# A Householder step with fewer matmuls, GpSimd rows and a planner that weighs layouts, in a four-layer graph network

## The chip, the cores and the metric

The kernel runs on one core of one Trainium2 chip. The metric is the device time of one execution in microseconds (us); three runs of the kernel before took 2328.39, 2328.72 and 2331.53 us. All data are float32. Of the engines, PE multiplies matrices (a matmul first loads one operand into the array as weights, then streams the other through it), DVE does vector arithmetic, ACT does functions and scaled copies, POOL (GpSimd) is a third vector engine, and SP issues DMAs.

## The reference, cut to what matters

Four layers run one after the other on x (128 batches x 64 nodes x 256 features) with one 64x64 graph matrix `adj`. The change touches the work that is done during layer 0.

```python
# layer 0: graph convolution, two products, two batch norms over all 8192 rows
h = relu(layernorm(x))
agg = einsum('nm,bmd->bnd', A_hat, h)                 # A_hat: adj + I, scaled
h = relu(batchnorm(agg @ W1.T + b1))                  # 256 -> 512
x = x + batchnorm(h @ W2.T + b2)                      # 512 -> 256
# layer 1: the eigenvectors of a 64x64 Laplacian of adj
L_norm = d_inv_sqrt[:, None] * (diag(deg) - A) * d_inv_sqrt[None, :]
_, U = eigh(L_norm)
h = relu(layernorm(x))
out = relu(einsum('mn,bnd->bmd', U.T, h) @ W1 + b1) @ W2 + b2
x = x + einsum('nm,bmd->bnd', U, out)
# layer 2: two graph products and four LSTMs; layer 3: attention over 512 edges
```

Layer 1 cannot start before the 64x64 eigenvectors U are known. They depend on `adj` alone, so they can be computed beside layer 0.

## The kernel before

**Two jobs at once.** `eigenvectors` runs layer 0 and the eigenproblem together. Layer 0 works on 16 blocks of 512 rows. In the hidden phase (`hidden_block`) a block is normalized by ACT, mixed with the graph by PE (`mix`, sixteen 128-wide matmul passes with the matrix `BDH`), multiplied by W1 (`product`, eight calls of 512 columns), and each result is copied out by ACT and given to DVE for batch statistics. After all 16 blocks the first batch norm's factors are known. Then the features phase (`features0`) goes over the 16 blocks again: ACT scales them, PE multiplies by W2 (eight calls of 512 columns a block), ACT copies out and squares. A float32 call of `matmul` appears in the trace as two MATMUL records, one for each of two passes.

**The eigenproblem.** `tridiagonal` reduces the 64x64 matrix A by 62 Householder steps (`householder`, c from 63 down to 2). After that `vectors` scales the result (`scale`), multiplies the reflectors together (`reflectors`), finds the eigenvalues by two rounds of a 32-step recurrence on DVE (`poly`, `values`), the vectors of the tridiagonal matrix (`twisted`), U itself, and a verdict (`verdict`) on which a branch is taken: where the verdict is bad, a slow solver runs in its place.

**One Householder step.** Each row is kept on all 64 partitions at once. `zy` makes two products with A: row c-1 of A (`z`) and A times column c (`y`), each a call with 64 weight columns. DVE and ACT form the reflection from the row x: norm by `square`, root `s0`, reciprocal `r`, `tt`, `nb`, then the corrected entries of x and the factor `KAP`. ACT makes `uk = KAP * x`; DVE makes `uA = z * nb + y`, the scalar `c2` (a sum over `uA * uk`), and `v = x * c2 - uA`. `outer` adds uk v' + v uk' in PSUM by two calls with one-row operands, and DVE adds it to A. The next row is made in two DVE operations from `uk`, `v` and `z`, without waiting for PE. A DMA on SP's queue stores each x row in `V`; x has a ring of 8 buffers.

**The planner.** `Plan` decides the order of the three engines' instructions when the program is built. `chain` places a step of the eigenproblem at once, at the time when its inputs are ready by the `busy` and `ready` numbers written beside it; before that, `fill` places waiting pieces of layer 0 (`beside`) on the same engine if they end no later than the slack of that engine after that time (`slack`: 0.6 us on PE, T; 0.3 on ACT, S; 0.3 on DVE, V). `emit` then issues everything in that order, and `Ordered` (line 799) ties each instruction of an engine behind the one before. So each engine runs its list strictly in order, and a late input holds up all that is behind it. Pieces of layer 0 that are left over when the 62 steps are placed (`rest`) are emitted after `vectors` and fill its gaps. The five PSUM banks of layer 0 are part of the plan.

All instructions that pass through `Ordered` carry line 799 in the profile, so they are told apart by their tiles: `ps` is layer 0's PSUM, `fps` and `fvps` that of the eigenproblem, and names that begin with `f_` are the eigenproblem's tiles.

Of the kernel before, what the change touches and what calls it, by code (L numbers as in the profile page):

```python
# [8 lines left out]
F32 = mybir.dt.float32  # L9
I32 = mybir.dt.int32  # L10
AF = mybir.ActivationFunctionType
ALU = mybir.AluOpType
# [772 lines left out]
GRID = 64  # L785

# [56 lines left out]
class Plan:  # L843
# [55 lines left out]

    def rest(self):  # L900

        while any(self.queue.values()):
            for e in self.queue:
                self.fill(e, 1e9)
# [8 lines left out]
class Fast:  # L913
# [31 lines left out]
    def sum(self, out, a, s, b, op0, op1=ALU.mult, name="junk"):  # L945

        w = a.shape[-1]
        j = self.t(f"{name}{a.shape[0]}", a.shape[0], 64)
        self.o.stt(j[:, 0:w], a, s, b, op0, op1, acc=out)
# [3 lines left out]
    def constants(self):  # L953
# [6 lines left out]
        self.P = t("P", 64, 1)  # L960
        iota(self.P[:], [[0, 1]], 0, 1)
# [21 lines left out]
        o.ts(self.low[:], self.J[:64, :], self.P[:], ALU.is_lt)  # L983
# [3 lines left out]
        o.copy(pi[:], self.P[:])  # L987
# [15 lines left out]
    def tridiagonal(self, S, made, plan):  # L1003
# [3 lines left out]
        A = self.A = t("A", 64, 64)  # L1007
# [3 lines left out]
        for x in (KAP, NB, V):  # L1011
            nc.vector.memset(x[:], 0.0)
        s0, r, tt, q, c2 = (t("h_" + x, 64, 1) for x in "s0 r t q c2".split())
        ja = t("ja", 64, 64)
        bc = lambda c, n=64: c.to_broadcast([n, 64])
        now = {}
        go = plan.chain

        def keep(name, a, b):
            now[name] = self.mm((a, b))  # L1020

        d = go("T", lambda: keep("p", S, self.JR[:]), [made], 0.3, 0.5)
        d = go("V", lambda: o.copy(m[:], now["p"][:]), [d], 0.15, 0.28)
        d = go("T", lambda: keep("p", self.JR[:], m[:]), [d], 0.3, 0.5)
        rest = go("V", lambda: o.copy(A[:], now["p"][:]), [d], 0.15, 0.28)
        d = go("T", lambda: keep("p", bc(ident[:64, 63:64]), A[:]), [rest], 0.3, 0.5)

        def first():
            x = now["x"] = self.rows.tile([64, 65], F32, name="f_x", bufs=8)
            o.copy(x[:, 0:63], now["p"][:, 0:63])  # L1030

        def square(w):
            x = now["x"]
            self.act(ja[:, 0:w], x[:, 0:w], AF.Square, accum_out=x[:, w:w + 1])

        row = go("V", first, [d], 0.15, 0.28)
        h = go("S", lambda: square(63), [row], 0.34, 0.42)
        for c in range(63, 1, -1):
            row, h, rest = self.householder(c, now, go, row, h, rest, (s0, r, tt, q, c2), square)

    def householder(self, c, now, go, row, h, rest, scalars, square):

        o, nc, t = self.o, self.nc, self.t
        ident = self.k.ident
        A, NB, OA, KAP, V = self.A, t("NB", 64, 64), t("OA", 64, 64, 2), t("KAP", 64, 64), t("V", 64, 64)
        s0, r, tt, q, c2 = scalars
        bc = lambda a, n=64: a.to_broadcast([n, 64])
        x = lambda a, b: now["x"][:, a:b]
        nb = NB[:, c - 1:c]
        e, w = 0.001 * c, c - 1  # L1050

        def zy():
            now["zp"] = self.ps.tile([64, 64], F32, name="fps")
            nc.tensor.matmul(now["zp"][:, 0:c], bc(ident[0:c, c - 1:c], c), A[0:c, 0:c], start=True, stop=True)
            now["yp"] = self.ps.tile([64, 64], F32, name="fps")
            nc.tensor.matmul(now["yp"][:, 0:c], bc(A[0:c, c:c + 1], c), A[0:c, 0:c], start=True, stop=True)

        def row_z():
            now["z"] = self.rows.tile([64, 64], F32, name="f_z")
            self.act(now["z"][:, 0:c], now["zp"][:, 0:c], AF.Copy)  # L1060

        def row_uk():

            nc.sync.dma_start(V[c:c + 1, 0:c], now["x"][0:1, 0:c])
            now["uk"] = self.rows.tile([64, 64], F32, name="f_uk")
            self.act(now["uk"][:, 0:c], x(0, c), AF.Copy, scale=KAP[:, c:c + 1])

        def row_uA():
            now["uA"] = self.rows.tile([64, 64], F32, name="f_uA")
            o.stt(now["uA"][:, 0:c], now["z"][:, 0:c], nb, now["yp"][:, 0:c], ALU.mult, ALU.add)  # L1070

        def row_v():
            now["v"] = self.rows.tile([64, 64], F32, name="f_v")
            o.stt(now["v"][:, 0:c], x(0, c), c2[:], now["uA"][:, 0:c], ALU.mult, ALU.subtract)

        def outer():
            uk, v = now["uk"], now["v"]
            p = now["p"] = self.ps.tile([64, 64], F32, name="fps")
            nc.tensor.matmul(p[0:c, 0:c], uk[0:1, 0:c], v[0:1, 0:c], start=True, stop=False)
            nc.tensor.matmul(p[0:c, 0:c], v[0:1, 0:c], uk[0:1, 0:c], start=False, stop=True)  # L1080

        def row_x():
            now["x"] = self.rows.tile([64, 65], F32, name="f_x", bufs=8)
            o.stt(x(0, w), now["uk"][:, 0:w], now["v"][:, w:c], now["z"][:, 0:w], ALU.mult, ALU.add)


        z = go("T", zy, [rest], 0.34, 0.42)
        sq = go("S", lambda: self.act(s0[:], x(c, c + 1), AF.Sqrt), [h], 0.13, 0.23)
        oa = go("S", lambda: self.act(OA[:, c, 1:2], x(c - 1, c), AF.Copy), [row], 0.12, 0.22)
        zs = go("S", row_z, [z], 0.15, 0.26 + e)  # L1090
        sg = go("V", lambda: o.ts(q[:], x(c - 1, c), **halve(0)), [row])
        d = go("V", lambda: o.recip(r[:], s0[:]), [sq])
        d = go("V", lambda: o.stt(tt[:], r[:], x(c, c + 1), s0[:], ALU.mult, ALU.add), [d, h])
        b = go("V", lambda: o.mul(nb, q[:], tt[:]), [d, sg])
        d = go("V", lambda: o.stt(x(c - 1, c + 1), OA[:, c, :], nb, x(c - 1, c + 1), ALU.mult, ALU.add), [b, oa])
        d = go("V", lambda: o.recip(KAP[:, c:c + 1], x(c, c + 1)), [d])
        uk = go("S", row_uk, [d], 0.16, 0.32 + e)
        d = go("V", row_uA, [zs, b, z], 0.12 + e, 0.25 + e)
        d = go("V", lambda: self.sum(c2[:], now["uA"][:, 0:c], 0.5, now["uk"][:, 0:c], ALU.mult), [uk, d],
               0.2 + e, 0.28 + e)  # L1100
        v = go("V", row_v, [d], 0.15 + e, 0.26 + e)
        p = go("T", outer, [v], 0.25, 0.45)
        if c > 2:
            row = go("V", row_x, [v], 0.15 + e, 0.22 + e)
            row = go("V", lambda: o.stt(x(0, w), now["v"][:, 0:w], now["uk"][:, w:c], x(0, w), ALU.mult, ALU.add),
                     [row], 0.15 + e, 0.25 + e)
            h = go("S", lambda: square(w), [row], 0.28 + e, 0.36 + e)
        rest = go("V", lambda: o.add(A[0:c, 0:c], A[0:c, 0:c], now["p"][0:c, 0:c]), [p], 0.12 + e, 0.22 + e)
        return row, h, rest

    def reflectors(self):
# [8 lines left out]
        self.sum(kc[:], self.KAPs[:], 1.0, ident, ALU.mult)  # L1120
# [22 lines left out]
    def scale(self):  # L1143

        o, nc, t = self.o, self.nc, self.t
        NB, A = t("NB", 64, 64), self.A
        self.KAPs = t("KAP", 64, 64)
        DM, NE = t("DM", 64, 64), t("NE", 64, 64)
        o.mul(DM[:], A[:], self.k.ident[:64, :64])
# [316 lines left out]
class Kernel:  # L1466
# [340 lines left out]
    def hidden_block(self, i, r, m, plan, needs, used):  # L1807
# [9 lines left out]
        def mix(dc):  # L1817
            p = now["m", dc] = psum.tile([P, BT], F32, name="ps")
            for j in range(TPB):
                self.mm(p[:, j * P:(j + 1) * P], now["h"][:, j, dc * P:(dc + 1) * P], self.BDH[:])  # L1820
# [966 lines left out]
```

## Time and profile before

| what | us |
|---|---|
| median of the three runs | 2328.72 |
| span of the profiled execution, first to last instruction | 2325.1 |
| 0 to 17: loads, graph matrix, first Householder step | 17 |
| 17 to 200: hidden phase beside Householder steps | 183 |
| 200 to 217: last hidden results, batch norm factors | 17 |
| 217 to 272: features phase beside the last Householder steps | 55 |
| 272 to 364.4: features phase beside the rest of the eigenproblem | 92.4 |
| 364.4 to 372: verdict's branch, then layers 1 to 3 | 7.6 |
| 372 to the end: layers 1 to 3 | 1953 |

The span ends 3.6 us below the median of the runs; what lies around it is not in the trace. The page's slices, each 58 us long, show how full the engines are; the first six and a half slices are the stage that is changed:

```profile
DVE  8887676888447777666767676559756686766667
ACT  5765865754436654433444444336435544444321
POOL 0000000000000000000000000000000000000000
PEclk9999999999999999999999999999999999999999
```

Each digit is the busy share in tenths. POOL is idle: over the whole span it has 26 instructions, nearly all of them fills and index patterns at the very start. The clock that PE was granted is nearly full everywhere.

One Householder step took between 2.8 and 6.3 us, 4.19 on the mean (from the starts of the operation that writes `f_h_q`, 11.8 for the first and 267.2 for the last: 255.4 us over 61 steps).

### The profile page before, as it was taken

How to read it: one execution, taken by the hardware profiler on the slowest of the kernel's cores; microseconds unless marked ns; L12 is line 12 of the kernel's file. 1: busy time of each engine (PE TensorE's matmuls, PEld its weight loads, DVE VectorE, ACT ScalarE, POOL GpSimd, SP SyncE). 2: the span in 40 equal slices, each digit the busy share in tenths (PEclk: the TensorE clock that was granted, in tenths of full speed). 3: DMA queues.
4: the chain of work that ended last, by engine and by line, in shares of the span. 5: the costliest groups of instructions: out<-in, count | busy, mean ns of one | idle time of the engine just before them, and what ended most of it. 6: DMA issues, size and time to landing. Idle time of an engine off the chain costs nothing.

```text
span 2325.1 us, 32725 instructions
## 1 busy us (share of the span) xinstructions
PE 2283.6 (98%) x12169; PEld 1633.1 (70%) x12169; DVE 1629.3 (70%) x4054; ACT 1139.5 (49%) x2483; POOL 3.0 (0%) x26
## 2 busy tenths in 40 slices
PE   7999998999999999999999999999999999999999
PEld 4554445676777788888999998888885544554544
DVE  8887676888447777666767676559756686766667
ACT  5765865754436654433444444336435544444321
POOL 0000000000000000000000000000000000000000
PEclk9999999999999999999999999999999999999999
DMA  5000211230000000001000002000010000000001
GB/s 171 1 1 26 65 56 30 71 83 19 1 37 0 1 19 1 1 1 37 1 1 1 1 1 73 1 1 17 1 46 28 1 5 15 15 19 14 14 24 46
DMA packets 61065, 54.81 MB, mean 24 GB/s; under 512 B 15203, under 2 KB 58724, under 8 KB 60900
## 3 DMA queue, kind: packets, MB, share of 16 engines
q1 hardware_dynamic: 60900, 52.66, 7.4%
q8 instruction: 97, 1.59, 0.3%
q14 instruction: 68, 0.56, 0.1%
HBM read 35.86 MB, written 16.78 MB: 23 GB/s over the span
## 4 chain that ended last, share of the span: by engine, by line
PE 79%; DVE 3%; issue 1%; ACT 1%; DMA 0%; SPq 0%; ACTq 0%; DVEq 0%
PE ps L799 69%; PE acc L799 5%; PE pt L799 4%; PE pe L799 1%; PE y L799 1%; DVE aw L799 1%; DVE X L799 1%; DVE sm_m L799 0%; DVE XV L799 0%; ACT ls_g L799 0%; ACT h L799 0%; DVE ls_g L799 0%; ACT big L799 0%; DVE ls_t L799 0%; DVE sm_e L799 0%
## 5 line engine op out<-in xcount | busy, mean ns | idle before, releaser
L799 ACT ACTIVATE ls_g<-ls_g,ls_b 128x512 f32<-128x512 f32 (+4 forms) x472 | 243.1, 565 | 151.4 <-DVE ls_g L799 149.6
L799 ACT ACTIVATE ls_g<-ps,ls_b 128x256 f32<-128x256 f32 (+3 forms) x268 | 115.5, 470 | 330.9 <-PE ps L799 327.7
L799 PE MATMUL ps<-z,w 128*128 128x512 f32 x512 | 254.9, 621 | 0.9 <-ACT z L799 0.9
L799 PE MATMUL ps<-big,X 128*128 128x176 f32 (+3 forms) x848 | 212.7, 366 | 0.1
L799 DVE TENSOR_TENSOR ls_g<-ls_z,ps 128x512 f32<-128x512 f32 (+5 forms) x256 | 146.8, 579 | 91.9 <-PE ps L799 90.4
L799 DVE TENSOR_TENSOR aw<-at,ed_OST 128x1024 f32<-128x1024 f32 x128 | 149.9, 1219 | 83.0 <-PE ps L799 82.8
L799 PE MATMUL ps<-ls_tx,X 128*128 128x160 f32 (+2 forms) x960 | 206.8, 326 | 0.6 <-ACT ls_g L799 0.6
L799 PE MATMUL ps<-X,X 128*128 128x160 f32 (+1 forms) x896 | 199.1, 306 | 0.0
L799 PE MATMUL ps<-X,ls_w 128*128 128x256 f32 x640 | 190.5, 379 | 0.0
L799 PEld LDWEIGHTS ps<-ls_tx,X 128*128 128x128 f32 x960 | 161.8, 190 | 15.1 <-DVE X L799 4.8
L799 PEld LDWEIGHTS ps<-big,X 128*128 128x128 f32 x848 | 145.9, 190 | 29.7 <-issue 19.4
L799 DVE TENSOR_TENSOR X<-ls_g 128x1024 f32<-128x1024 f32 (+2 forms) x108 | 117.4, 1087 | 49.9 <-ACT ls_g L799 49.8
L799 ACT ACTIVATE r<-ps 128x512 f32<-128x512 f32 x256 | 131.6, 614 | 41.5 <-PE ps L799 41.4
L799 PEld LDWEIGHTS ps<-X,X 128*128 128x128 f32 x896 | 148.4, 190 | 0.0
L799 PE MATMUL ps<-X,ls_s 128*128 128x256 f32 x480 | 142.3, 379 | 0.0
L799 PEld LDWEIGHTS ps<-z,w 128*128 128x128 f32 x512 | 87.2, 190 | 69.0 <-issue 60.2
L799 PE MATMUL ps<-ls_tx,ls_s 128*128 128x256 f32 x464 | 134.8, 379 | 0.0
L799 PE MATMUL ps<-ed_S,Q 64*128 64x512 f32 x512 | 132.9, 618 | 1.4 <-DVE hT L799 0.7
L799 PE MATMUL ps<-ls_tx,ls_w 128*128 128x256 f32 x464 | 133.2, 380 | 0.0
L799 PEld LDWEIGHTS ps<-X,ls_w 128*128 128x128 f32 x640 | 121.4, 190 | 16.8 <-DVE X L799 0.3
L799 PE MATMUL ps<-big,ls_w 128*128 128x256 f32 x464 | 131.9, 379 | 0.7 <-ACT ls_z L799 0.7
L799 PE MATMUL ps<-aw,ed_ODT 128*64 128x512 f32 x512 | 117.3, 595 | 0.1
(545 smaller groups left out, 4019.0 us busy)
## 6 DMA issues: line engine op xcount, KB each, us to landing
X<-in_x_dram SPq DMA_DIRECT2D x32, 512.0 KB
xs<-X SPq DMA_DIRECT2D x16, 512.0 KB
X<-xs SPq DMA_DIRECT2D x16, 512.0 KB
out_dram<-X SPq DMA_DIRECT2D x31, 256.0 KB
X<-in_L_gnn_Wih_t_dram SPq DMA_DIRECT2D x4, 512.0 KB
ls_w<-in_L_gnn_Wih_t_dram SPq DMA_DIRECT2D x4, 512.0 KB
ls_w<-in_L_gnn_Whh_t_dram SPq DMA_DIRECT2D x4, 512.0 KB
w<-in_L_gnn_W_t_dram SPq DMA_DIRECT2D x2, 512.0 KB
```

The source lines that it names most:

```text
L799: i = method(*a, **kw)
```

## The change

The planner gets a method `weigh`. It builds the plan of one Householder step with each of 27 sets of slacks (0.2, 0.45, 0.8 on PE; 0.1, 0.3, 0.6 on ACT; 0.1, 0.35, 0.65 on DVE), rates each by the busy time that it placed (weight 1 on PE, 0.5 on ACT, 2 on DVE) less 2.7 times the time at which the step's results are ready, takes the state back, and plans the step once more with the best set. All of this happens while the program is built.

The step's arithmetic is laid out anew. z and y come from one matmul call whose weights `ex` hold two blocks of 64 columns: a column of the identity, written by GpSimd, and the masked column of the new A, written by DVE straight from PSUM (`m`). The rank-two update is one call with 65-row operands: row 0 of `left` holds uk and row 64 of `right` holds uk, both written by GpSimd; row 64 of `left` holds -uA, also by GpSimd; rows 0 to 63 of `right` hold v, written by DVE. It is uneven because v now carries the whole scalar `dd`, and the other side carries uA alone. `tt` goes; `qh` (DVE) and `qs` (ACT) come. `uk` is no longer an input of the sum. The ring of x has 6 buffers in place of 8, and z, uk and uA one each in place of two.

In layer 0 the calls of W1 and W2 are cut into halves of 256 columns and the mix into two pieces of two tiles, with the planner's times to match.

```diff
+R = 65
...
+    def weigh(self, make, slacks, worth, cost):
+        free, queue = dict(self.free), {e: list(v) for e, v in self.queue.items()}
+        n, k = len(self.steps), len(self.opened)
+        best = None
+        for slack in [*slacks, None]:
+            self.slack = slack or best[1]
+            made = make()
+            if slack is None:
+                return made
+            gain = sum(x.busy * worth.get(x.engine, 0.0) for x in self.steps[n:])
+            gain -= cost * max(x.at + x.ready for x in made)
+            if best is None or gain > best[0]:
+                best = gain, slack
...
+        self.MK = t("MK", 64, 64)
+        o.ts(self.MK[:], self.J[:64, :], self.P, ALU.is_gt)
...
+        self.left, self.right = ([t(f"{n}{i}", R, 66) for i in range(2)] for n in ("L", "R"))
+        self.ex = [t(f"EX{i}", R, 2, 64) for i in range(2)]
+        for x in (*self.left, *self.right, *self.ex):
+            nc.gpsimd.memset(x[:], 0.0)
...
+            row, h, rest = plan.weigh(lambda: self.householder(c, now, go, row, h, rest),
+                                      self.slacks, dict(T=1.0, S=0.5, V=2.0), 2.7)
...
+    def unit(self, c):
+        self.nc.gpsimd.tensor_copy(self.ex[c % 2][0:64, 0, :], self.k.ident[0:64, c - 1:c].to_broadcast([64, 64]))
...
-        def zy():
-            now["zp"] = self.ps.tile([64, 64], F32, name="fps")
-            nc.tensor.matmul(now["zp"][:, 0:c], bc(ident[0:c, c - 1:c], c), A[0:c, 0:c], start=True, stop=True)
-            now["yp"] = self.ps.tile([64, 64], F32, name="fps")
-            nc.tensor.matmul(now["yp"][:, 0:c], bc(A[0:c, c:c + 1], c), A[0:c, 0:c], start=True, stop=True)
+        def products():
+            zy = now["zy"] = self.ps.tile([P, 64], F32, name="fps")
+            nc.tensor.matmul(zy[:, 0:c], ex[c % 2][:].rearrange("p a b -> p (a b)"), A[:, 0:c], start=True, stop=True)
...
+        def side(out, a, scale):
+            nc.gpsimd.tensor_scalar(out, a[0:1, 0:c], scale, None, op0=ALU.mult)
...
         def outer():
-            nc.tensor.matmul(p[0:c, 0:c], uk[0:1, 0:c], v[0:1, 0:c], start=True, stop=False)
-            nc.tensor.matmul(p[0:c, 0:c], v[0:1, 0:c], uk[0:1, 0:c], start=False, stop=True)
+            p = now["p"] = self.ps.tile([P, 64], F32, name="fps")[:R]
+            nc.tensor.matmul(p[:, 0:c], left[:, 0:R], right[:, 0:c], start=True, stop=True)
...
-        d = go("V", lambda: o.stt(tt[:], r[:], x(c, c + 1), s0[:], ALU.mult, ALU.add), [d, h])
-        b = go("V", lambda: o.mul(nb, q[:], tt[:]), [d, sg])
+        g = go("V", lambda: o.mul(qh[:], q[:], x(c, c + 1)), [sg, h], 0.09, 0.25)
+        d = go("V", lambda: o.recip(r[:], s0[:]), [sq], 0.09, 0.25)
+        qr = go("S", lambda: self.act(qs[:], s0[:], AF.Copy, scale=q[:]), [sq, sg], 0.13, 0.25)
+        b = go("V", lambda: o.stt(nb, r[:], qh[:], qs[:], ALU.mult, ALU.add), [d, g, qr], 0.09, 0.25)
...
+        uA = go("V", row_uA, [b, zy, zs], 0.12 + e, 0.25 + e)
+        k = go("V", lambda: o.recip(kap, x(c, c + 1)), [d], 0.09, 0.25)
+        uk = go("S", row_uk, [k], 0.16, 0.32 + e)
+        sides = [go("P", lambda: side(left[64:65, 0:c], now["uA"], -1.0), [uA], 0.15, 0.4)]
+        sides += [go("P", lambda out=out: side(out, now["x", c], KAP[0:1, c:c + 1]), [k], 0.15, 0.4)
+                  for out in (left[0:1, 0:c], right[64:65, 0:c])]
+        d = go("V", lambda: self.sum(dd[:], now["uA"][:, 0:c], kap, x(0, c), ALU.mult), [uA, k], 0.2 + e, 0.28 + e)
+        v = go("V", lambda: o.stt(right[0:64, 0:c], x(0, c), dd[:], now["uA"][:, 0:c], ALU.mult, ALU.subtract),
+               [d], 0.12 + e, 0.26 + e)
...
+            row = go("V", row_x1, [uk], 0.12 + e, 0.26 + e)
...
+        p = go("T", outer, [v] + sides, 0.25, 0.45)
...
+            m = go("V", lambda: o.stt(ex[w % 2][0:64, 1, :], now["p"][0:64, w:c].to_broadcast([64, 64]), A[0:64, w:c],
+                                         self.MK[:, w:c].to_broadcast([64, 64]), ALU.add, ALU.mult), [p], 0.12, 0.25)
         rest = go("V", lambda: o.add(A[0:c, 0:c], A[0:c, 0:c], now["p"][0:c, 0:c]), [p], 0.12 + e, 0.22 + e)
+        if c > 3:
+            go("P", lambda: self.unit(c - 2), [zy], 0.15, 0.4)
...
-            plan = Plan(dict(T=0.6, S=0.3, V=0.3), 5)
+            plan = Plan(dict(T=0.6, S=0.3, V=0.3, P=0.0), 5)
...
-            x = beside("T", lambda dc=dc: mix(dc), h, 0.98, 1.1, bank)
+            x = beside("T", lambda dc=dc: mix(dc, 0), h, 0.5, 0.6, bank)
+            x = beside("T", lambda dc=dc: mix(dc, 1), [x], 0.5, 0.66)
...
-            x = beside("T", lambda hc=hc: product(hc, 0), mixed, 0.86, 0.9, bank)
-            x = beside("T", lambda hc=hc: product(hc, 1), [x], 0.86, 1.0)
+            x = beside("T", lambda hc=hc: product(hc, 0, 0), mixed, 0.43, 0.43, bank)
+            for k, kc in ((0, 1), (1, 0), (1, 1)):
+                x = beside("T", lambda hc=hc, k=k, kc=kc: product(hc, k, kc), [x], 0.43, 0.6 if k and kc else 0.43)
...
-                for kc in range(4):
-                    x = beside("T", lambda oc=oc, kc=kc, f=product: f(oc, kc), [z[kc]] + ([x] if x else []), 0.86, 1.0,
-                               None if kc or x else bank)
+                for k in range(2):
+                    for kc in range(4):
+                        x = beside("T", lambda oc=oc, k=k, kc=kc, f=product: f(oc, k, kc), [z[kc]] + ([x] if x else []),
+                                   0.43, 0.6, None if kc or x else bank)
```

## The prediction, made before the changed kernel was run

> **What bounds the kernel now.** I began with the page's slices, which say that PE is nearly always busy, and went on to the windows of layer 0's own matmuls (tile `ps`) by stage, since a busy PE only says that records lie close together. The changed code runs in the first 364 us; everything later takes U and x and is the same in both kernels. This view has, for each stretch, its length and then busy time and number of instructions by engine:
>
> ```profile
> 17.00:200.00 183.00, 156.72 (x500) 73.42 (x501) 41.03 (x60) 53.63 (x92) 1.00 0.10 30
> 200.00:217.00 17.00, 14.78 (x70) 8.67 (x68) 2.79 (x4) 2.39 (x4) 0.92 0.00 0
> 217.00:272.00 55.00, 48.05 (x94) 15.46 (x94) 1.40 (x2) 14.31 (x40) 1.00 0.26 76
> 272.00:364.40 92.40, 76.76 (x163) 28.54 (x162) 0.00 (x0) 28.09 (x80) 1.00 0.16 47
> ```
>
> The first bracket counts PE's records: layer 0 still had 163 of them to do when the last Householder step ended near 272. Then I read one step in the order of PE's time (start, duration, engine):
>
> ```profile
> 102.60 1.45 PE L799 MATMUL ps<-z,w 128*128 128x512 f32 x3
> 103.98 0.27 PE L799 MATMUL fps<-f_v,f_uk 1*44 1x44 f32 x2
> 104.09 0.25 PE L799 MATMUL fps<-f_uk,f_v 1*44 1x44 f32 x2
> 104.26 1.13 PE L799 MATMUL ps<-z,w 128*128 128x512 f32 x2
> 105.32 0.31 PE L799 MATMUL fps<-f_A,ident 43*64 43x43 f32 x2
> 105.46 0.29 PE L799 MATMUL fps<-f_A 43*64 43x43 f32 x2
> 105.67 1.55 PE L799 MATMUL ps<-z,w 128*128 128x512 f32 x3
> ```
>
> Durations overlap, so I use start to start. A 512-wide pass takes 0.429 us (eight from 100.35 need 3.63 up to 103.98, less 0.20 for the change). `outer` holds PE 0.28 us (103.98 to 104.26), `zy` 0.35 (105.32 to 105.67). The two passes between them need 0.86 but 1.06 goes by: each change from layer 0 to the eigenproblem and back loses 0.20. A step costs PE about 0.28 + 0.35 + 2 x 0.20 = 1.03 at this c, 0.98 on the mean of all.
>
> The sum from layer 0's first pass (17.3) to the verdict's matmul (364.3) is 347 us:
> - layer 0: 512 passes of 0.429, 256 + 56 narrow ones (mix, and the fills of the batch norm's gap) of 0.109: 253.
> - 62 steps of 0.98: 61.
> - the rest of the eigenproblem after 272, read in the same way: 26.
> - the remainder, 7, is PE standing; listing the holes gives about 12, 9 of them before 272 (1.5 before 197.4, 1.3 at 200 under a lower clock, 3 in the steps at 93.7, 114.3 and 215.9, in which no layer 0 work lay between the two visits) and 3 at 334 and 348; the steps without layer 0 work saved some changes in return.
>
> So **PE is the bound of this stage**, not the length of the Householder chain. Both end together, but only because the planner stretches a step: the chain by its own hops (start to start where nothing stood between: square 0.35, root 0.23, `r` 0.20, `tt` 0.24, `nb` 0.26, x 0.24, KAP 0.24, `uk` 0.36, sum 0.24, v 0.29, two row operations 0.58) needs 3.2 us, and a step takes 4.19. PE waits for nothing in between.
>
> **The change part by part.**
>
> *One call in place of two for z and y.* The saving seems obvious: half the calls. But the one call has 128 weight columns where two had 64 each. The trace has such shapes elsewhere:
>
> ```profile
> 358.94 0.43 PE L799 MATMUL fvps<-U,I 64*128 64x64 f32 x2
> 359.30 0.70 PE L799 MATMUL ps<-z,w 128*128 128x512 f32 x1
> ...
> 313.15 0.38 PE L799 MATMUL fps<-f_v_L,f_I 64*128 64x1 f32 x2
> 313.46 1.13 PE L799 MATMUL ps<-z,w 128*128 128x512 f32 x2
> ...
> 279.74 0.32 PE L799 MATMUL fps<-f_VT 64*64 64x64 f32 x2
> 279.99 1.12 PE L799 MATMUL ps<-z,w 128*128 128x512 f32 x2
> ```
>
> With 128 weight columns a call holds PE 0.36 us at 64 streamed columns and 0.31 at one; `zy` took 0.37 at c = 60 and 0.32 at c = 2. **PE gains nothing**: 62 x 0.01, under 1 us.
>
> *One call for the update.* 65 weight columns and 65 rows are nearest to the third pair: 0.25 at 64 columns, less 0.05 for short ones as above. Before, `outer` took from 0.36 (c = 61) to 0.17 (c = 2). Mean 0.23 against 0.24: again under 1 us. Together -1.
>
> *The chain.* `tt` and `uk` leave the path from row to row: 0.24 + 0.36, and one of the two row operations (`row_x1`) no longer waits for v: 0.29. So 3.2 becomes 2.3. The other loop (update, `m`, add to A, `products`, `zs`, `uA`, sum, v) adds to about 2.1 to 2.6 by the same hops, as `m` comes in front of the add. I expect steps of 2.8 to 3.6 us and an end of the 62 steps near 200 to 235 instead of 272. It buys little: the passes of layer 0 that no longer fit between the steps run after them. The gain would be the whole 37 to 70 us only if PE had nothing left to do.
>
> *More work on DVE and ACT.* Per step one DVE operation more (`m`, some 0.27, near `uA`'s 0.25; `qh` replaces `tt`), one more on ACT (`qs`, near OA's 0.19). Hidden under PE's time: DVE is 80% busy in the hidden phase and ACT 67%. Without cover it is 0.27 + 0.1 a step on the chain, which still leaves it under 3 us.
>
> *GpSimd rows.* Three one-row operations a step, two needed with v by `outer`, and `unit` beside. No POOL operation of this kind is in the trace. Nearest: the affine select that reads and writes 128 elements, 0.30 us; a fill of 1 to 4 elements 0.09; below. A row has 32 elements on the mean, so I take 0.2, with 0.09 and 0.56 (an index pattern of 512) as ends. They follow each other on POOL: three need 0.6, and a hand-over as between DVE and ACT (0.23) gives 0.85 after uA; sum and v need 0.55. The planner counts 0.7.
>
> ```profile
> 1.11 0.30 POOL masks.py:199 TENSOR_SCALAR_AFFINE_SELECT ident<-ident 128x128 f32<-128x128 f32 x1
> ```
>
> Here a rule speaks against the change. The Trainium skill, "SBUF — State Buffer", section "Who interferes with whom", says that a DVE instruction with two SBUF inputs and a GpSimd instruction that reads SBUF exclude each other: the later one waits for the whole of the other. The sum and v are such instructions and run just when the rows are copied. By the row alone the rows cost the chain 0.15 beyond the plan; by the rule DVE also waits about 2 x 0.2, 0.55 in all, 34 us over 62 steps if it lay open. No overlap of the two engines is in this trace. What covers it: the planner books 0.25 + 0.25 of PE for a step, and the trace shows 0.97, so PE will run 0.47 us a step later than planned, and a chain that is up to that much late makes no hole. I take 0 to 5 us, and 1 for the sum.
>
> *A ring of six.* The ring of x shrinks to 6, and the SP queue frees it: the first row's DMA into V stands behind the loads and starts at 34.88. The seventh row reuses its slot. Six steps of about 4 us from 11.5 (these first ones carry statistics on DVE) come to 35: a wait of 0 to 3, I take 1. Single buffers for z, uk and uA are read out within a step: 0. The fills of the new tiles run before the graph matrix is ready (8.66): 0.
>
> *Finer pieces.* 512 passes become 1024 of 256 columns. These run at 0.215 in layer 2 (twelve in 2.75 us with the last one's tail): 512 x (2 x 0.215 - 0.429) = +1. In return a visit of the eigenproblem waits behind a piece of 0.43 in place of 0.86. The 27 layouts cost nothing on the chip.
>
> *Holes.* With a shorter chain the visits' inputs come earlier, and I take it that 6 of the 9 us of holes up to 272 close (an estimate: two thirds); those of 334 and 348 belong to later code.
>
> **Sum:** calls -1, GpSimd rows +1, ring +1, pieces +1, holes -6: -4 us. On the execution profiled 2325.1 becomes 2321; with the 3.6 us around it, **2324.5** against the median 2328.7.
>
> **Rivals.**
> - *Slower: the GpSimd rows set the step.* Place: `outer`, first in PE's queue with all of layer 0 behind it. If a row takes d, it is ready 3d + 0.25 after uA, 0.7 is planned and 0.47 absorbed: the point is d = 0.31 us. At 0.4 PE stands 0.28 a step, 17 us, so 2342; at 0.56 far more, +47. For it: the lock, and the weights, which reward short steps and so plan no reserve. Against: the 0.30 row moved four times as much.
> - *More: PE's holes all close.* All 12 us instead of 6, -10 us in all: 2318.6; the 2 us of costs gone as well: 2316. For it: the list of holes; against: two lie behind matmuls of the unchanged part. PE cannot give more.
> - *The gap between the phases loses its cover.* Now 202 to 217 holds four steps. If steps are 3 us, 62 of them are over before the hidden phase, and the gap falls among `poly`'s operations on DVE. Then 5 to 10 us of PE are empty: 2335.
> - *It does not do what it says*: the uneven update upsets the verdict and the slow solver runs. Nothing in the trace tells; the time would be beyond any range here.
>
> **How the numbers follow.** PE's sum 0.50 (own range 2317 to 2333), GpSimd rows 0.27, all holes 0.11, uncovered gap 0.10, slow solver 0.02. The range that keeps 8 in 10: 2313 to 2350. I call 0.2% (4.7 us) the least difference that can be told. PE's sum gives 0.25 faster, 0.21 same, 0.04 slower; the holes add 0.11 faster; the gap 0.02 same, 0.08 slower; the rows 0.01 same, the rest slower. Rounded: faster 0.36, same 0.24, slower 0.40.
>
> **What would show it.** Right: the last `f_h_q` well before 267, `products` holding PE 0.31 to 0.36 and `outer` 0.20 to 0.25, layer 0's last pass still near 360. Wrong: PE waiting for POOL or DVE before `outer`, steps over 3.8 us, or the verdict's branch starting well before 355, which would mean that PE was never the bound.

## The result and the profile after

| | median, us | range |
|---|---|---|
| before | 2328.66 | 2328.39 to 2331.53 |
| changed | 5582.39 | 5580.53 to 5584.05 |

The ratio is 2.3971 (95% interval 2.3937 to 2.4004). From the page of the kernel before, the busy time by engine:

```profile
PE 2283.6 (98%) x12169; PEld 1633.1 (70%) x12169; DVE 1629.3 (70%) x4054; ACT 1139.5 (49%) x2483; POOL 3.0 (0%) x26
```

And from the page of the changed kernel the span, the same row, two rows of slices and the costliest group:

```profile
span 5580.8 us, 57110 instructions
...
PE 2359.0 (42%) x12738; PEld 1775.8 (32%) x12738; DVE 4338.0 (78%) x23282; ACT 1317.7 (24%) x3353; POOL 85.8 (2%) x282
...
PE   8871100000000000000000000099999999999999
...
PEclk9985555555555555555555555599999999999999
...
L122 PE MATMUL eps<-e_left,e_ones 64*64 64x1 f32 x2 | 0.4, 252 | 2179.3 <-DVE e_left L45 2179.3
```

DVE has 23282 instructions where it had 4054, and the tiles `e_...` belong to the slow solver: **the verdict came out bad and the branch of the slow solver ran**. The windows of all engines show how long (length, then busy time and instructions of PE, its weight loads, DVE, ACT and POOL, then PE's clock):

```profile
10.00:384.00 374.00, 331.74 (x1733) 266.90 (x1733) 287.61 (x1431) 248.81 (x811) 81.78 (x248) 0.98 0.15 44
384.00:3626.00 3242.00, 83.97 (x321) 46.59 (x321) 2690.32 (x19173) 166.04 (x814) 0.11 (x1) 0.50 0.00 0
3626.00:5580.00 1954.00, 1942.16 (x10682) 1461.60 (x10681) 1353.30 (x2631) 901.41 (x1727) 0.63 (x3) 1.00 0.06 18
```

The middle row is 3242 of the 3254 us. It has 19173 DVE instructions, and PE is busy for 84 us of it. The rows of layer 0's matmuls (tile `ps`), in the stretches that the prediction used, say that the first stage did not get shorter either:

```profile
17.00:200.00 183.00, 149.72 (x708) 118.94 (x709) 39.72 (x58) 50.86 (x88) 0.97 0.11 30
200.00:217.00 17.00, 12.79 (x49) 9.15 (x48) 2.65 (x4) 3.42 (x6) 0.80 0.01 1
217.00:272.00 55.00, 43.24 (x193) 30.20 (x192) 3.50 (x5) 8.31 (x23) 1.00 0.14 39
272.00:364.40 92.40, 78.01 (x324) 58.46 (x323) 0.00 (x0) 28.12 (x84) 1.00 0.22 63
```

PE's time with layer 0 between 17 and 272 us fell from 219.6 to 205.8 us (sums of the first three rows), its clock from 0.92 to 0.80 in the second row and from 1.00 to 0.97 in the first. The last Householder step ends near 280 instead of 272, and a step takes 4.38 us instead of 4.19. So there are two questions: why the verdict fell, and what the changed schedule costs without the slow solver.

### The profile page after: what moved, and what is told of

Read it like the earlier page. It is cut to its first block, busy times and chain, and to the rows that moved or that the text cites. A ratio compares the mean times of both kernels' runs of the same rounds, so it can differ in the third digit from the quotient of the medians.

```text
span 5580.8 us, 57110 instructions
## 1 busy us (share of the span) xinstructions
PE 2359.0 (42%) x12738; PEld 1775.8 (32%) x12738; DVE 4338.0 (78%) x23282; ACT 1317.7 (24%) x3353; POOL 85.8 (2%) x282
## 5 line engine op out<-in xcount | busy, mean ns | idle before, releaser
L457 ACT ACTIVATE e_q_r_y<-e_q_r_hh 64x1 f32<-64x1 f32 x540 | 109.6, 203 | 1357.3 <-DVE e_q_r_hh L51 1234.7
L800 PE MATMUL ps<-z,w 128*128 128x256 f32 x1024 | 259.3, 399 | 0.2
L68 DVE RECIPROCAL e_q_r_r<-e_q_r_y 64x1 f32<-64x1 f32 x540 | 83.6, 155 | 153.6 <-ACT e_q_r_y L457 150.9
L800 PEld LDWEIGHTS ps<-z,w 128*128 128x128 f32 x1024 | 189.9, 195 | 25.3 <-ACT z L800 1.4
L800 PEld LDWEIGHTS ps<-big,X 128*128 128x128 f32 x848 | 146.0, 190 | 29.7 <-issue 19.4
```

Source lines behind the costliest of these rows:

```text
L68: self.v.reciprocal(o, a)
L457: nc.scalar.activation(y[:], hh[:], AF.Sqrt)
L800: i = method(*a, **kw)
```

## Why the slow solver ran: ten kernels

Theory L: only the rounding of the tridiagonal matrix changed. In `twisted` each eigenvector is built outward from one row r, the one with the smallest |g|. g is made of ratios of float32 determinants, which for some eigenvalues cancel to exact zeros towards the end of the recurrence; then row 0 can have g = 0 by accident and be chosen although the vector has next to nothing there. Rival D: the uneven update, or a row written by GpSimd, makes the vectors inexact for good.

The first kernel multiplies the verdict by zero (`o.ts(li[:], p[:], 0.0, ALU.mult)` in place of the copy), so that the slow solver never runs.

> The changed kernel with its verdict multiplied by zero, so the vectors of the fast solver are used whatever the tests say (left out: the decision itself; the tests still run). Theory A, the +3254 us are the slow solver and nothing else: the time falls to near the kernel before. The last matmul of the verdict starts at 371.5 us in the profile of the changed kernel and at 364.35 in that of before, and nothing behind it was changed, so 2328.7 + 7.2 = 2336, between 2332 and 2341. Theory B, something outside the slow solver (the layers behind, the clock) pays too: more than 2345. The prediction's own sum, without the slow solver: 2324.5.

Measured: 2344.23 us (2341.18 to 2346.03) against 2326.56, ratio 1.0067 (1.0049 to 1.0084). The 3240 us are the slow solver, as theory A said. The number is 3 us over its interval, since I had read the wrong landmark. The output of this kernel is off by 0.047 (relative error), so the vectors were really bad, and the verdict was not merely too strict. The verdict's matmul moved from 364.35 to 373.66, but layer 0's last pass, which came just before it, now comes after it: 383.7 instead of 363.8. What follows starts at 392.8 instead of 373.5.

The next two leave the verdict in force. One swaps the factors of one sum in one step:

```diff
-self.sum(dd[:], now["uA"][:, 0:c], kap, x(0, c), ALU.mult)
+self.sum(dd[:], x(0, c), kap, now["uA"][:, 0:c], ALU.mult)     # c == 20 alone
```

> The changed kernel with the two factors of one sum swapped in one of the 62 steps (c = 20: x * kap * uA in place of uA * kap * x); same instructions, same order, other rounding in the last bits. Theory L, the verdict falls by a rounding accident in one row of the twisted factorization: another rounding draws another lot, the fast vectors pass, and the time is that of the held verdict, 2332 to 2341. Theory D, the uneven update (asymmetric halves, rows through GpSimd) costs accuracy in a lasting way, or a row is wrong: one swapped product in one step cannot mend it, 5582.

The other keeps row 0 from being chosen:

```diff
         o.mabs(g[:], g[:])
+        nc.vector.memset(g[:, 0:1], 8.0)
         o.red(gm[:], g[:], ALU.min)
```

> The changed kernel with one instruction more: the column 0 of g, the measure by which a vector's twist row is chosen, is set to 8, so that row 0 is never chosen. Theory L says which accident it is: for one eigenvalue the determinants of the reversed sequence have rounded to exact zeros, g of row 0 is an exact 0.0, and row 0 is chosen though this vector has hardly anything there; barred, the verdict passes and the time is that of the held verdict within 0.5 us, 2332 to 2341. Theory D: the vectors are inexact as a whole, the verdict stays bad, 5582.

Measured: 2346.51 us (one run) and 2345.58 us (2344.1 to 2345.9, ratio 1.0075, 1.0059 to 1.0092), both above their 2332 to 2341 by the same wrong landmark. Neither mends any accuracy of the update, and both bring the kernel back. So D falls for this data, and the bar says which accident it is: the choice of row 0. From here on "the mended kernel" is the one with the bar. That g was an exact zero there is argued from the arithmetic; no run read it out.

If L holds, the kernel before has been living with the same risk. Its twin adds the two products of the row update in the other order in one step:

```diff
-o.stt(x(0, w), now["uk"][:, 0:w], now["v"][:, w:c], now["z"][:, 0:w], ALU.mult, ALU.add)
+o.stt(x(0, w), now["v"][:, 0:w], now["uk"][:, w:c], now["z"][:, 0:w], ALU.mult, ALU.add)   # c == 50 alone
```

and the second operation takes the other product.

> The kernel before, with the two products of its row update added in the other order in one of the 62 steps (c = 50); same instructions, same order, other rounding. Theory L: the kernel before holds the same lot, and this ticket may lose, too; if it does, near 2328 + 3250 = 5578. Theory D, only the uneven update is inexact: 2328 to 2332. A fast time here does not tell against L, one slow time tells against D.

> The kernel before with the swapped products in step 50, which took 5565 us, and row 0 barred as twist row. If the kernel before falls by the same accident as the changed one, the bar brings it back: 2325 to 2335. If its vectors are bad for another reason: 5565.

Measured: **5564.92 us**, and with the bar 2331.31 (one run each). The kernel before falls by the same accident after one swapped sum, with no uneven update and no GpSimd row in it.

Whether the changed update is more exposed was tried with more draws of either kind, all without the bar: factors swapped in all, the even or the odd steps.

> The changed kernel, no bar, with the two factors of the sum dd swapped in all 62 steps. Equal lots (rounding decides, and the uneven update is no more exposed than the symmetric one): a minority of the five draws of this batch falls, on whichever side. The uneven update is more exposed: the draws of the changed kernel fall, those of before do not. Fast is 2340 to 2350 here, slow 5582.

> As the run before, swapped in the steps with an even c alone. Fast is 2340 to 2350, slow 5582; equal lots: a minority of the five draws; more exposed: this one is slow.

> As the run before, swapped in the steps with an odd c alone. Fast is 2340 to 2350, slow 5582; equal lots: a minority of the five draws; more exposed: this one is slow.

> The kernel before, no bar, with the two products of its row update added in the other order in the steps with an even c. Fast is 2325 to 2335, slow 5565. Equal lots: a minority of the five draws of this batch falls, on whichever side; the uneven update more exposed: this one is fast.

> As the run before, in the steps with an odd c. Fast is 2325 to 2335, slow 5565. Equal lots: a minority of the five draws falls; the uneven update more exposed: this one is fast.

Measured, one run each: changed 5576.3, 2346.51 and 5577.44; before 2328.44 and 2331.85. Neither theory's pattern came out: two of these five fell, both of the changed kernel, yet its even swap did not. With the earlier ones, three of five roundings of the changed kernel fell and one of four of the kernel before. So few draws cannot tell the two apart, and the swaps are not independent, since a swapped product often rounds to the same bits. This stays open.

## What the schedule costs: the other eight kernels

Mended, the change still costs 17 to 19 us. All of it lies in the first stage: layer 0's last pass comes 19.5 us later (383.3 for 363.8) and the end 18.6 us later (spans 2343.7 and 2325.1). PE's idle time before a matmul up to 384 us, by what ended it (total, times, longest), for the mended kernel and then, up to 364 us, for the kernel before:

```profile
PE fps L800 <- POOL f_R L1112: 20.4, 34, 2.6
PE fps L800 <- DVE f_h_q L800: 8.5, 14, 1.2
```

```profile
PE fps L799 <- DVE f_v L799: 3.7, 4, 1.4
PE fps L799 <- DVE m_m L799: 3.0, 2, 2.4
```

The update's matmul stands in PE's queue for a time at which GpSimd's rows are not written. These are their durations (min/median/max in ns, mended kernel):

```profile
L1112 POOL TENSOR_SCALAR f_L<-f_uA x62: 213/296/397, 13.6 to 282.9; 1x63 f32<-1x63 f32 x1, 1x62 f32<-1x62 f32 x1, 1x61 f32<-1x61 f32 x1, 1x60 f32<-1x60 f32 x1
L1112 POOL TENSOR_SCALAR f_L<-f_x,f_KAP x62: 283/432/520, 14.1 to 283.2; 1x63 f32<-1x63 f32 x1, 1x62 f32<-1x62 f32 x1, 1x61 f32<-1x61 f32 x1, 1x60 f32<-1x60 f32 x1
L1112 POOL TENSOR_SCALAR f_R<-f_x,f_KAP x62: 286/369/546, 14.6 to 283.6; 1x63 f32<-1x63 f32 x1, 1x62 f32<-1x62 f32 x1, 1x61 f32<-1x61 f32 x1, 1x60 f32<-1x60 f32 x1
```

The three of a step add to 1.09 us on the mean. The planner counts 0.7 from the first one's start to the last one's result. And this is PE around one such wait in the changed kernel (start, duration; in brackets the idle time and its releaser):

```profile
125.09 0.31 PE L800 MATMUL fps<-f_A,f_EX 65*128 65x39 f32 x2
125.23 2.03 PE L800 MATMUL ps<-BDH,z 128*128 128x128 f32 x16
128.11 0.31 PE L800 MATMUL fps<-f_R,f_L 65*65 65x39 f32 x2 [0.84 <-POOL f_R L1112]
129.10 0.39 PE L800 MATMUL fps<-f_A,f_EX 65*128 65x38 f32 x2 [0.68 <-DVE f_h_q L800]
129.31 4.96 PE L800 MATMUL ps<-z,w 128*128 128x256 f32 x14
134.11 0.26 PE L800 MATMUL fps<-f_R,f_L 65*65 65x38 f32 x2
```

Three things are to be seen.
- PE stands 0.84 us for GpSimd, then 0.68 more, since no piece of layer 0 lies between the update and the next products; nine steps of the mended kernel are like that (8.4 us from update to products; four and 2.3 us before).
- After the holes the fourteen passes take 4.80 us, 0.343 each instead of 0.215: the granted clock was 0.50 for 3.4 us of them. Before that stood 3.4 us with PE busy for 1.89 (length, PE's busy time and instructions, clock):

```profile
126.56:129.97 3.41, 1.89 (x14) 1.00 0.00 0
129.97:133.39 3.42, 3.42 (x10) 0.50 0.00 0
```

- Where nothing is late, `products` holds PE for 0.14 us (125.09 to 125.23) and `outer` for 0.08 to 0.09 (134.11 to the next pass at 134.19).

The last point was not in the prediction. The sum for PE from the eigenproblem's first matmul (8 us) to layer 0's last pass, start to start, is this (us; a visit is a stretch of the eigenproblem's matmuls, with the idle time inside it; the last column is the kernel e12 below):

| | before | mended | e12 |
|---|---|---|---|
| layer 0's passes at full length | 253.0 | 254.2 | 253.0 |
| between passes of layer 0 beyond that | 18.9 | 23.8 | 17.5 |
| gap before a visit of the eigenproblem | 20.6 | 41.7 | 36.1 |
| the visits themselves | 63.2 | 55.4 | 47.1 |
| sum | 355.7 | 375.1 | 353.7 |

An unhindered visit (median) cost 0.094 + 0.242 for `outer` and 0.093 + 0.341 for `zy` in the kernel before, gap and hold. In the mended kernel it is 0.001 + 0.089 and 0.001 + 0.142. **Unhindered, the new calls free 62 x 0.54 = 33 us of PE** (an estimate from these medians: in the mended kernel fewer than half of the visits came in time), and the waits took more than that. The table shows the balance, 19.4 us more.

Four kernels then undo one suspect each. The first only tells the planner what the trace shows:

```diff
-sides = [go("P", lambda: side(left[64:65, 0:c], now["uA"], -1.0), [uA], 0.15, 0.4)]
+sides = [go("P", lambda: side(left[64:65, 0:c], now["uA"], -1.0), [uA], 0.3, 0.5)]
-sides += [go("P", lambda out=out: side(...), [k], 0.15, 0.4)
+sides += [go("P", lambda out=out: side(...), [k], 0.4, 0.6)
-    go("P", lambda: self.unit(c - 2), [zy], 0.15, 0.4)
+    go("P", lambda: self.unit(c - 2), [zy], 0.24, 0.45)
```

> The mended kernel (row 0 barred), in which the planner counts what GpSimd's rows really take by the profile of the mended kernel (0.30, 0.42 and 0.38 us on the mean): busy 0.3 and 0.4 in place of 0.15, ready 0.5 and 0.6 in place of 0.4, and 0.24 for the unit tile. The work is the same, only the order changes. Theory G, the +17 us left after the mend are PE standing before the update's matmul, since it was put into PE's queue for a time at which GpSimd's rows are not done (20.4 us in 34 waits): these waits fall under 5 us, steps may get longer without harm, and the time is 2344 less 15 to 20: 2324 to 2330. Theory F, the loss is in the finer pieces and the many changes: still 2340 or more.

Measured: 2333.0 us (2330.99 to 2336.81) against 2329.18, ratio 1.0020 (1.0012 to 1.0027). With the work unchanged, 12.6 of the mended kernel's 2345.6 us are gone, though not all that G gave. (In the sets of runs here the kernel before had medians from 2326.5 to 2329.2, so a difference between two sets is good to a few us; the ratios, 1.0075 and 1.0020, say 13.) Its waits:

```profile
PE fps L800 <- DVE f_h_q L800: 8.9, 19, 0.9
PE fps L800 <- POOL f_R L1112: 8.5, 17, 1.3
```

The waits for GpSimd are 8.5 us, not under 5; those for DVE before `products` have not moved.

The second takes the rows from GpSimd:

```diff
-nc.tensor.matmul(p[:, 0:c], left[:, 0:R], right[:, 0:c], start=True, stop=True)
+nc.tensor.matmul(p[:, 0:c], self.uk[0:1, :], right[0:1, 0:c], start=True, stop=False)
+nc.tensor.matmul(p[:, 0:c], self.nu[:], self.uk[0:1, 0:c], start=False, stop=True)
```

with `nu` = -uA made by ACT.

> The mended kernel without GpSimd's rows: the update as two matmuls of one row each from uk, v and -uA, where they stand in row 0; the -uA row is written by ACT; GpSimd keeps the unit tile. Theory G: PE's waits for GpSimd (20.4 us) go, two calls hold PE as long as the one did (0.24 us against 0.23), so 2344 less 17 to 22: 2322 to 2327, and no later than the kernel before. Theory F: 2340 or more.

Measured: 2340.06 us (2338.83 to 2342.14), ratio 1.0042 (1.0028 to 1.0056): G's number was missed by 13 us, and this is the edge of theory F's "2340 or more", though not by its mechanism. The waits for GpSimd are gone (the gaps before visits fall from 41.7 to 23.7 us), but my price of the two calls was wrong. PE in one step of this kernel:

```profile
108.15 0.31 PE L800 MATMUL fps<-f_R,f_uk 1*64 1x44 f32 x2
108.29 0.28 PE L800 MATMUL fps<-f_uk,f_nu 1*64 1x44 f32 x2
108.50 1.13 PE L800 MATMUL ps<-z,w 128*128 128x256 f32 x4
```

From 108.15 to 108.50 PE is held for 0.35 us, and unhindered visits of this kind have a gap of 0.094 in front again. With 65 rows it was 0.09 in all, so 62 x 0.35 = 22 us of PE came back in place of the waits.

The other two change the size of layer 0's pieces: the old size in the mended kernel, and the new size alone in the kernel before.

> The mended kernel with layer 0's matmuls in the pieces of the kernel before (512 columns, pairs of 0.86 us). Theory G: a visit that comes too early stands the same, and one that comes late waits longer behind a piece: 2342 to 2350. Theory F, 1024 pieces and their joints cost: 2330 to 2338.

> The kernel before with nothing but the finer pieces of layer 0. By the prediction's term (512 x (2 x 0.215 - 0.429) = +1 us, shorter waits of the visits -1 to -3): 2325 to 2330. Theory F: slower than 2333.

Measured: 2334.87 us (2332.35 to 2339.11), ratio 1.0027 (1.0021 to 1.0034), as theory F had it: whole pieces save 10.7 us. And 2333.02 (2329.91 to 2334.4), ratio 1.0016 (1.0009 to 1.0024): alone, the finer pieces cost 3.8 us. That is above the 2325 to 2330 of the prediction's term and nearly four times its +1, and it just reaches theory F's 2333. In that profile the passes are 1.2 us longer, the time between passes grows from 18.9 to 22.8, and what was to come back in shorter waits does not.

The weighing of layouts was taken out of the mended kernel by its own slack values of before:

```diff
-row, h, rest = plan.weigh(lambda: self.householder(c, now, go, row, h, rest),
-                          self.slacks, dict(T=1.0, S=0.5, V=2.0), 2.7)
+row, h, rest = self.householder(c, now, go, row, h, rest)
```

> The mended kernel with the fixed slacks of the kernel before (0.6 for PE, 0.3 for ACT and DVE, 0 for GpSimd) in place of the 27 layouts weighed in each step. Theory W, the weighing rewards short steps and so leaves no reserve: it is the cause of the steps without any pass of layer 0 between update and products (9 of them, 8.4 us, in the mended kernel) and of most early visits: 2326 to 2333. Theory G, the planner's belief in 0.15 us a row is the cause whatever the slack: the waits for GpSimd stay near 15 to 20 us and the time is 2336 to 2345.

Measured: 2382.74 us (2381.95 to 2383.97), ratio 1.0240 (1.0225 to 1.0256). **Both theories missed, and in the other direction**: with these durations in the planner, the weighing was worth 37 us. Waits for GpSimd rose to 46.3 us, and of the small operations from batch norm's statistics to its factors (224 to 231 us in the mended kernel) three ran at 213 to 219 us and the rest only from 279.5 to 282, behind the last step. So the last 15 steps ran without layer 0. Windows of all engines:

```profile
220.00:230.00 10.00, 6.13 (x51) 5.49 (x50) 6.75 (x42) 3.99 (x20) 3.59 (x11) 1.00 0.00 1
240.00:250.00 10.00, 2.90 (x12) 2.35 (x12) 6.72 (x42) 4.12 (x21) 3.43 (x12) 0.50 0.00 0
290.00:300.00 10.00, 10.00 (x36) 6.12 (x37) 4.14 (x15) 5.55 (x12) 0.00 (x0) 0.53 0.18 52
```

PE is busy for 2.9 of 10 us, at half its clock, and in the third row, fully busy again, it still has only 0.53. What of the 37 us is due to the missing layer 0, to the waits and to the clock was not separated.

Last, the edits that helped were put together: both of them; then, of GpSimd's three rows, the one that stays in partition 0 given to ACT, with whole pieces and with fine ones.

```diff
-sides += [go("P", lambda out=out: side(...), [k], 0.4, 0.6) for out in (left[0:1, 0:c], right[64:65, 0:c])]
+sides += [go("P", lambda: side(right[64:65, 0:c], now["x", c], KAP[0:1, c:c + 1]), [k], 0.4, 0.6),
+          go("S", lambda: self.act(left[0:1, 0:c], now["x", c][0:1, 0:c], AF.Copy, scale=KAP[0:1, c:c + 1]), [k], 0.16, 0.32 + e)]
```

> The mended kernel with both edits that helped alone: the planner is told GpSimd's real durations (2344 to 2333) and layer 0's pieces are whole again (2344 to 2335). If they act on different losses (waits for GpSimd there; joints, and holes at a low granted clock, here), they add: 2321 to 2327. If both only stretch the plan and so close the same holes: 2330 to 2334.

> As the run before, and of GpSimd's three rows the one that stays in partition 0 (uk) is written by ACT, which takes about 0.2 us and stands beside. GpSimd's two rows then need 0.68 us after uA where sum and v need 0.55 and their hand-overs 0.3, so that update no longer waits for them: PE's waits for GpSimd under 3 us, 1 to 5 us below the run before, 2318 to 2325. If ACT's one row more delays z or the square, no gain: within 1.5 us of it.

> The mended kernel with uk's row by ACT and the planner told GpSimd's durations, but with the finer pieces of layer 0 kept. If the pieces cost by themselves (joints and holes, +4 us in the kernel before): 2326 to 2332, slower than the same with whole pieces (2323.8). If whole pieces only helped where visits were late: 2322 to 2325.

Measured: 2330.33 us (2328.27 to 2335.27; ratio 1.0018, 1.0009 to 1.0027). That is the number for edits that close the same holes, but the trace shows another reason: PE's sum did fall, to 345.9 us, and layer 0's last pass comes at 354.1, while the verdict's matmul comes at 370.9. Here the chain of the eigenproblem had become the bound. With uk's row on ACT both end together again (361.9 and 364.5): **2323.75 us (2321.82 to 2326.89) against 2326.48, ratio 0.9985 (0.9975 to 0.9994)**. This gain of 0.15% is less than the 0.2% that the prediction called distinguishable, though its interval excludes 1. With fine pieces it is 2337.46 (2335.45 to 2338.27; ratio 1.0039, 1.0027 to 1.0051), 13.7 us slower than with whole ones, which is beyond what I had expected from either theory: by the same sum, 5.5 us more between passes and 7.8 more in the visits, whose idle time grew. PE's waits in the best of them, up to 364 us:

```profile
PE fps L800 <- DVE f_h_q L800: 12.7, 23, 1.4
PE fps L800 <- POOL f_R L1112: 6.4, 7, 1.4
```

Not under 3 us for GpSimd, as I had said, and the waits for DVE's operations before `products` are now the larger part.

## Why the prediction was wrong

**The step that failed** is the last rival, "It does not do what it says: the uneven update upsets the verdict and the slow solver runs. Nothing in the trace tells", with a chance of 0.02 and no price other than "beyond any range here". The runs showed in its place that the slow solver took 3242 of the 3254 us, and that it ran since row 0 was chosen as twist row: barred, the kernel takes 2345.58. The trace could not price a branch that was not taken, but the code shows a whole second solver behind it, and nothing stood behind the 0.02. Nor was the chance a matter of the uneven update's accuracy. A change of rounding in front of the verdict can turn it: the kernel before falls, too, once one sum is turned round (5564.92 us). The trace shows the branch as it fell for one set of bits; that says nothing of how far from the edge it fell.

**The sum without the slow solver** was 2324.5 (its terms, -4 from 2328.7, make 2324.7) and came out at 2345.6:
- *GpSimd rows, +1.* d was taken as 0.2 us, and it is 0.30, 0.42 and 0.38 on the mean (with the factor from a number, and from a tile). The rival that was named for this had the point at 0.31, 17 us of PE at 0.4 and 2342 in all: the place and the size were right (20.4 us of waits), at a chance of 0.27. That its total came so near was luck: the same sum left out what PE gained by the new calls and what the pieces and the half clock cost. The argument against it, "the 0.30 row moved four times as much", looked at the wrong thing: a fixed part carries most of the price (0.21 to 0.29 us for the shortest rows). Telling the planner the durations took 12.6 us away.
- *Finer pieces, +1.* +3.8 alone and +10.7 to +13.7 with the new steps. I had counted the passes' length, and neither the time between them nor the visits.
- *One call in place of two: "PE gains nothing".* A visit in time costs PE 0.54 us less a step, 33 in all by the estimate above. The calls that I took (128 weight columns, 0.36 and 0.31; 64 columns, 0.25) have 64 rows of contraction; the new ones have 65 rows and at least 65 weight columns.
- *The chain: steps of 2.8 to 3.6 us and an end at 200 to 235.* 4.40 us in the mended kernel, end near 283. A step is as long as the planner and the waits make it.
- *Holes, -6.* They grew: the gap before visits went from 20.6 to 41.7 us, and with it came half-clock stretches. Of the clock's windows of 10 us up to the last pass, those below 1.00 lose 8.5 us in the mended kernel (0.83, 0.95, 0.88, 0.83 and 0.66) and 1.7 in the one before.
- *The lock between DVE and GpSimd*, weighed in the prediction by the Trainium skill's "SBUF — State Buffer", did not show. The 62 v operations took 245 ns on the mean in the mended kernel, 59 of them beside a GpSimd row, and 243 in e6, which has no such row. The sum takes 243 ns in the mended kernel and 241 in e6, so the rise from 176 in the kernel before is not GpSimd's doing. The 0.4 us a step by that rule did not come. Whether GpSimd's rows are stretched in return was not tried.
- *PE as the bound* held in the kernel before, in the mended one and in e12, whose ends follow PE's sum; in e11 it was the chain. In "what would show it", PE waiting for POOL before `outer` and steps over 3.8 us were named as the signs of a wrong sum, and both came.
- *The gap between the phases* did not lose its cover in the changed kernel. It did in e10, where the whole price was 37 us rather than 5 to 10, with longer waits and a half clock in it.

## What to carry to other kernels

Before pricing an edit of arithmetic, look for a branch behind it that is decided by data: price the other side, and draw a few other roundings before trusting either kernel. In a queue that runs strictly in order, a duration that a planner takes too short is paid by the engine that is the bound; read it from the trace and write it in before judging the idea. And price a small matmul by its gap and its hold, from a call on the same side of 64 in contraction rows and in weight columns, with the same neighbour.

## What the runs showed of the hardware

- **65 against 64.** Between passes of 128 rows, a call with 65 rows and 65 or 128 weight columns had a gap of 0.001 us in front and held PE 0.089 or 0.142 us. Calls with 64 rows or fewer, one-row ones too, had 0.094 and 0.24 to 0.35, in the same profiles. Rows are not the whole of it: a call with 128 rows and 64 weight columns had the gap of 0.094 as well (two passes of 0.215, and the call 0.53 after the first one's start; mended kernel):

```profile
309.64 0.59 PE L800 MATMUL ps<-z,w 128*128 128x256 f32 x2
310.17 0.68 PE L800 MATMUL fvps<-f_SG,f_I2T 128*64 128x64 f32 x8
```

  The Trainium skill, "TensorEngine Tiling (Array Packing)", section "Key Properties", says that changing the tiling mode drains TensorE. That fits: the small calls may run in another mode than their neighbours. No run here shows the mode itself. It is in no part of the prediction.
- **A late 65-row call loses a part of this.** With a wait in front, it held PE 0.14 and 0.215 us (medians, mended kernel).
- **The clock halves after short holes.** In the changed kernel, idle times of 0.84 and 0.68 us between 127.3 and 129.1 us were followed by 3.4 us at 0.50. Its half-clock stretches up to 300 us start at 130.0, 167.5, 181.2 and 208.5, which is 11, 4 and 8 times 3.41 us apart, and last 3.41 us or twice that. In the 3.41 us before each start PE was busy for 1.89, 1.56, 1.96 and 1.48 us; one other such window after 21 us, with 1.96, had no half clock behind it. In the mended kernel the four windows after 20 us with 1.57 to 1.98 us of work had it, and those with 2.08 and more had not. So the share of work in a window fits these two traces, and not the length of a single hole: a little over half was too little. The limit is not sharp, since in e6 one such window had 0.71 of its length in work. In e10, with PE 2.4 to 3.4 of 10 us busy, the clock went to 0.50 at 231 us, though no hole was longer than 2.9 us, and stayed there to 299 us, the last 15 us with PE fully busy. The skill's "TensorE: Matmul & The Clock Gate", section "What's actually happening", gives two clocks and a free-running window of about 3.4 us, and both agree with the trace. It lets the clock fall after an idle window and rise after a busy one. Here windows with PE busy for half of them were enough to lower it, and in e10 one busy window did not raise it; the measurement decides.
- **A one-row GpSimd operation costs 0.3 to 0.4 us on the mean.** From 63 elements down to 2 it falls from 0.40 to 0.21 for a row scaled by a number, and from 0.46 or 0.48 to about 0.28 for one scaled from a tile.
